# A graph layer: masks and inverse roots on VectorE instead of GpSimd, per-node work behind the second product

## The chip, the cores and the metric

One core of a Trainium2 chip. The metric is device microseconds of one execution, the median of the runs in the fast state; all runs of this study were in that state but one of b_order, 468.86 us, which the record marks as slow and which is left out. The kernel before takes 458 us. Engines: PE is TensorE, DVE is VectorE, ACT is ScalarE, POOL is GpSimd.

## The reference, cut to what matters

Two graph layers over N = 3327 nodes of 64 features, with a dense 0/1 adjacency matrix in fp32:

```python
h = jnp.maximum(_layernorm(x), 0.0)
x = x + gnn_0(h, adj)       # for every pair (i, j): sigmoid * adj * logmap(h_i, h_j), summed over j;
                            # then for every node: expmap, proj
h = jnp.maximum(_layernorm(x), 0.0)
mask = (adj != 0)
rank = jnp.cumsum(mask, axis=1)             # how many neighbours lie behind j
w = mask * where(pos > 0, 0.5 ** (k - pos), 0.0)
x = x + (w @ (h @ weight) + bias)
# ... (the hyperbolic functions are cut)
```

The first layer costs one 3327 x 3327 set of pair products. The second needs a running count of neighbours over the same matrix, so both are done in one sweep. Between them lies a stage on each node alone: three inverse roots, one tanh and some sixty operations on 4 to 8 values in each partition, a dozen more on 256 to 512.

## The kernel before

The sweep has four strips of columns, of 8, 8, 6 and 4 blocks of 128 nodes, in 91 rounds (26, 26, 26 and 13). One round, in the order of the program:

```python
STRIPS = [(0, 8), (8, 8), (16, 6), (22, 4)]
ON_ACT = ((1, 5), (4, 7), (2, 3), (1, 2))    # share of the reads of pc that ACT takes, by strip
PORTIONS, LAST = (2, 5, 5, 16), 6            # node-stage work let through in a round, by strip; LAST: behind a decode
BIG, LATER = 4, 99                           # a wide instruction counts 4, a small one 1
# ...
            total(n - 2)                                        # PE: sum of the products, fp32
            A.activation(pq, pq, AF.Gelu, scale=-WG / QS)       # ACT: two passes over the pair products
            A.activation(pq, pq, AF.Gelu, scale=WH)
            # ...
            V.scalar_tensor_tensor(sg, sg, 1.0, ad_of.pop(n)[:, :w], op0=ALU.add, op1=ALU.mult)  # "first product"
            edges(m + 1)            # the mask: G.tensor_scalar(mask, ad, 0.0, None, op0=ALU.is_equal)
            count(m, js(m)[-1])     # PE: neighbour count from the masks, into pc
            sigmoids(n + 1)         # ACT
            read(m, js(m)[-1])      # pc -> 8 bits, by ACT or by DVE
            products(n + 1)         # PE: pair products, into pq
            advance(PORTIONS[k])    # a portion of the node stage of the strip before
            if lo == 0:
                for _ in steps:     # last round of a strip: whatever is left of it
                    pass
            # ...
            V.scalar_tensor_tensor(sg, pq, WD, sg, op0=ALU.add, op1=ALU.mult)                    # "second product"
```

The node stage is a generator: each `yield` says what it just issued counts for. Its roots start on POOL, then take one refining step on DVE:

```python
G.tensor_tensor(y, v, nhalf[:, :n], op=ALU.pow)
V.tensor_scalar(g, v, -0.5, None, op0=ALU.mult)
yield LATER
# ... three dependent DVE instructions
```

Behind the sweep comes the tail: 26 decodes of the counts ("wt", alternately DVE and ACT), the products of the second layer on them, and, in portions behind the decodes, the node stage of the last strip. The products of the last four blocks need its result.

## Time and profile before

The median is 458.52 us (457.63 to 458.9, 3 runs). By stages, cut at the first "first product" of each strip and at DVE's copy-out of the last strip's sums:

| start | strip 0 | strip 1 | strip 2 | strip 3 | tail |
|---|---|---|---|---|---|
| 47.2 us | 89.3 | 106.6 | 87.0 | 61.2 | 65.1 |

Two of the rows by slices, each digit the busy tenths of a fortieth of the span:

```profile
DVE  4893899999999799998999999999889999789821
POOL 8910699887897697695968787959877541014000
```

DVE is full almost to the end. POOL's digits are high too, but a busy engine is a bound only if another waits for it.

### The profile page before, as it was taken

Reading aid. Unit: us, or ns where it says so; the run is one execution under the profiler, and the core shown is the slowest. Engines: PE = TensorE matmul, PEld = TensorE weight load, DVE = VectorE, ACT = ScalarE, POOL = GpSimd, SP = SyncE. Lnnn points to the kernel's source line nnn. Section 1 sums busy time; section 2 is a strip of 40 time slices with the busy share of each in tenths; the row PEclk is TensorE's granted clock in tenths of the full one; section 3 lists DMA queues with packets and bytes.
Section 4 is the critical chain, followed back from the end, with each engine's and each line's share of the span. In section 5 each row is a group of like instructions: output and inputs, shape, how many; then the busy total and the mean of one; then the engine's idle time right before and its main releaser. Section 6 shows DMA issues by size and latency. Waiting matters only on the chain.

```text
span 456.4 us, 4831 instructions
## 1 busy us (share of the span) xinstructions
PE 368.4 (81%) x1460; PEld 155.6 (34%) x1460; DVE 393.1 (86%) x660; ACT 369.9 (81%) x399; POOL 289.7 (63%) x137
## 2 busy tenths in 40 slices
PE   0336799999998989879889988698778689678973
PEld 0034233333333323323334444343332232233453
DVE  4893899999999799998999999999889999789821
ACT  1647989999999899887899999779798689577930
POOL 8910699887897697695968787959877541014000
PEclk9997999999998999998999999989899899999987
DMA  7402455545555343444236444336443100000002
GB/s 201 201 12 62 136 157 170 166 141 155 154 194 157 110 130 105 143 130 138 73 102 182 119 123 136 103 106 175 146 124 102 53 1 0 1 0 1 1 21 62
DMA packets 23313, 48.98 MB, mean 107 GB/s; under 512 B 8713, under 2 KB 9169, under 8 KB 23279
## 3 DMA queue, kind: packets, MB, share of 16 engines
q1 hardware_dynamic: 20993, 47.66, 35.0%
q10 hardware_dynamic: 2062, 0.87, 0.9%
q0 software_dynamic: 224, 0.07, 0.3%
q8 instruction: 13, 0.21, 0.2%
q14 instruction: 21, 0.17, 0.1%
HBM read 46.40 MB, written 0.87 MB: 104 GB/s over the span
## 4 chain that ended last, share of the span: by engine, by line
PE 34%; DVE 32%; ACT 20%; issue 7%; DMA 2%; POOL 2%; DVEq 0%; ACTq 0%; POOLq 0%
PE po L993 14%; DVE sg L1077 8%; DVE sg L1058 7%; ACT pq L1048 4%; PE pq L983 4%; ACT wt L1100 4%; ACT sg L976 4%; PE pq L984 4%; PE pc L956 4%; PE pc L955 4%; ACT pq L1049 3%; PE pw L1107 2%; DVE behind_lo L969 2%; DVE behind_hi L969 2%; DMA w_lr<-in_w_att 2%
## 5 line engine op out<-in xcount | busy, mean ns | idle before, releaser
L944 POOL TENSOR_SCALAR mask<-ad 128x1024 bf16<-128x1024 f32 (+1 forms) x91 | 254.5, 2801 | 81.9 <-PE pc L955 57.8
L993 PE MATMUL po<-sg,hw 128*65 128x512 f32 (+1 forms) x364 | 161.7, 568 | 1.6 <-DVE sg L1077 1.3
L1058 DVE SCALAR_TENSOR_TENSOR sg<-sg,ad 128x1024 f32<-128x1024 f32 (+1 forms) x91 | 112.6, 1237 | 6.6 <-ACT sg L976 6.5
L1077 DVE SCALAR_TENSOR_TENSOR sg<-pq,sg 128x1024 f32<-128x1024 f32 (+1 forms) x91 | 103.8, 1141 | 2.7 <-ACT pq L1049 1.5
L1048 ACT ACTIVATE pq<-pq 128x1024 f32<-128x1024 f32 (+1 forms) x91 | 86.7, 952 | 20.3 <-PE pq L984 14.9
L976 ACT ACTIVATE sg<-left_b,right 128x1024 f32<-128x1024 f32 (+2 forms) x104 | 100.5, 980 | 0.0
L1049 ACT ACTIVATE pq<-pq 128x1024 f32<-128x1024 f32 (+1 forms) x91 | 86.2, 947 | 2.9
L955 PE MATMUL pc<-mask,ca 128*128 128x512 bf16 (+1 forms) x175 | 66.5, 380 | 23.4 <-DVE behind_hi L969 8.3
L983 PE MATMUL pq<-iu,ju 71*128 71x512 f16 (+1 forms) x182 | 68.7, 377 | 17.0 <-DVE sg L1077 16.3
L956 PE MATMUL pc<-mask,cb 128*128 128x512 bf16 (+1 forms) x182 | 67.7, 382 | 12.6 <-POOL mask L944 11.1
L993 PEld LDWEIGHTS po<-sg,hw 128*65 128x65 f32 x364 | 49.9, 139 | 72.8 <-issue 56.4
L984 PE MATMUL pq<-iz,jz 128*128 128x512 f16 (+1 forms) x182 | 67.5, 378 | 3.8 <-DMA iz<-jz 3.8
L1107 PE MATMUL pw<-wt,s 128*128 128x512 bf16 (+1 forms) x182 | 40.4, 371 | 10.2 <-ACT wt L1100 7.0
L956 PEld LDWEIGHTS <-cb 128*128 128x128 bf16 x182 | 18.2, 100 | 74.2 <-issue 54.3
L969 DVE TENSOR_SCALAR behind_hi<-pc,none 128x1024 uint8<-128x1024 f32 (+2 forms) x26 | 28.2, 1084 | 6.9 <-PE pc L956 6.7
L969 DVE TENSOR_SCALAR behind_lo<-pc,none 128x1024 uint8<-128x1024 f32 (+2 forms) x26 | 29.0, 1115 | 5.1 <-ACT pq L1049 2.6
L967 ACT ACTIVATE behind_hi<-pc,none 128x1024 uint8<-128x1024 f32 (+2 forms) x26 | 24.6, 945 | 8.0 <-PE pc L956 7.9
L983 PEld LDWEIGHTS <-ju 71*128 71x128 f16 x182 | 18.3, 100 | 36.8 <-DVE sg L1077 18.0
L967 ACT ACTIVATE behind_lo<-pc,none 128x1024 uint8<-128x1024 f32 (+2 forms) x26 | 23.9, 919 | 7.8 <-PE pc L956 7.8
L517 POOL TENSOR_TENSOR rn<-t,nhalf 128x8 f32<-128x8 f32 (+2 forms) x8 | 13.7, 1709 | 25.1 <-DVE t L770 22.4
L984 PEld LDWEIGHTS <-jz 128*128 128x128 f16 x182 | 18.3, 101 | 31.2 <-issue 12.0
L1107 PEld LDWEIGHTS <-s 128*128 128x128 f16 x182 | 17.8, 100 | 30.3 <-issue 11.6
(227 smaller groups left out, 302.7 us busy)
## 6 DMA issues: line engine op xcount, KB each, us to landing
ad<-in_adj_t SPq DMA_DIRECT2D x65, 512.0 KB, 3.6
ad<-in_adj_t SPq DMA_DIRECT2D x26, 384.0 KB, 3.2
out<-o SPq DMA_DIRECT2D x6, 128.0 KB, 1.9
left_b<-left_d SPq DMA_DIRECT2D x1, 512.0 KB, 4.7
x_sb<-in_x ACTq DMA_DIRECT2D x1, 416.0 KB, 5.7
x_sb<-in_x SPq DMA_DIRECT2D x1, 416.0 KB, 5.0
left_b<-left_d SPq DMA_DIRECT2D x1, 384.0 KB, 4.1
iz<-jz ACTq DMA_DIRECT2D x2, 128.0 KB, 2.3
```

Source lines behind the costliest of these rows:

```text
L944: G.tensor_scalar(*args, 0.0, None, op0=ALU.is_equal)
L955: T.matmul(S.pc[:, f0:f1], ca, S.before[:, f0:f1], start=False, stop=True, skip_group_check=True)
L956: T.matmul(S.pc[:, f0:f1], cb, now[:, f0:f1], start=S.first, stop=True, skip_group_check=True)
L969: V.tensor_scalar(kept, S.pc[:, : S.F], rest, 0.0, op0=ALU.add, op1=ALU.max)
L976: A.activation(part(n, sg, j), S.left[:, : S.F], AF.Tanh, bias=right[:, j : j + 1], scale=0.5)
L983: T.matmul(part(n, pq, j, f0, f1), ju[:KB, j, :], S.iu[:, f0:f1], start=True, stop=False)
L984: T.matmul(part(n, pq, j, f0, f1), jz[:, j, :], S.iz[:, f0:f1], start=False, stop=True)
L993: T.matmul(S.po[: D + 1, f0:f1], hw[:, j, :], part(n, sg_of[n], j, f0, f1), start=j == NB - 1, stop=j == 0)
L1048: A.activation(pq, pq, AF.Gelu, scale=-WG / QS)
L1049: A.activation(pq, pq, AF.Gelu, scale=WH)
L1058: V.scalar_tensor_tensor(sg, sg, 1.0, ad_of.pop(n)[:, :w], op0=ALU.add, op1=ALU.mult)
L1077: V.scalar_tensor_tensor(sg, pq, WD, sg, op0=ALU.add, op1=ALU.mult)
```

## The change

The intent: take the masks off POOL, whose work disturbs DVE through the memory port that the two share; keep the node stage in one place; and let PE have the second product sooner, by placing the node stage's portion behind it. To pay for the masks on DVE, ACT takes more of the reads. The diff, cut to its core:

```diff
-ON_ACT = ((1, 5), (4, 7), (2, 3), (1, 2))
+ON_ACT = ((1, 2), (5, 8), (3, 4), (1, 2))
-PORTIONS, LAST = (2, 5, 5, 16), 6
+PORTIONS, LAST = (2, 4, 4, 8), 8
 # ... masks: 1 where there is an edge, so the counting weights change sign and a bias tile goes
-        G.tensor_scalar(*args, 0.0, None, op0=ALU.is_equal)
+        V.tensor_scalar(*args, 0.0, None, op0=ALU.not_equal)
-            V.tensor_scalar(kept, S.pc[:, : S.F], rest, 0.0, op0=ALU.add, op1=ALU.max)
+            V.tensor_scalar(kept, S.pc[:, : S.F], 0.0, None, op0=ALU.max)
 # ... each root: 11 dependent DVE instructions instead of POOL's power and 4 on DVE
+        for _ in range(3):
+            E.tensor_mul(t, y, y)
+            E.scalar_tensor_tensor(t, v, -0.5, t, op0=ALU.mult, op1=ALU.mult)
+            E.scalar_tensor_tensor(y, t, 1.5, y, op0=ALU.add, op1=ALU.mult)
 # ... ACT's three steps of the node stage wait for the next round, behind its Gelus
+            asked_of_act()
 # ... the portion behind the second product
-            advance(PORTIONS[k])
-            if lo == 0: ...
-            V.scalar_tensor_tensor(sg, pq, WD, sg, op0=ALU.add, op1=ALU.mult)
+            if hi - lo > 1:
+                advance(PORTIONS[k])
+            V.scalar_tensor_tensor(sg, pq, WD, sg, op0=ALU.add, op1=ALU.mult)
+            advance(PORTIONS[k])
+            if lo == 0: ...
```

The node stage has 76 small DVE instructions in the new form, 59 in the old. The new code also holds an unused branch ("hidden") that puts these small instructions on POOL in another form.

## The prediction

> **What bounds the kernel now.** I read the page first, then the instructions by form, then the busy time of each engine in five stretches cut at the first "sg<-sg,ad" of each strip, then the instructions in order of time. The page's first rows give two engines near the span and POOL far below it; its groups show the work that the change moves:
>
> ```profile
> PE 368.4 (81%) x1460; PEld 155.6 (34%) x1460; DVE 393.1 (86%) x660; ACT 369.9 (81%) x399; POOL 289.7 (63%) x137
> ...
> L944 POOL TENSOR_SCALAR mask<-ad 128x1024 bf16<-128x1024 f32 (+1 forms) x91 | 254.5, 2801 | 81.9 <-PE pc L955 57.8
> ...
> L1058 DVE SCALAR_TENSOR_TENSOR sg<-sg,ad 128x1024 f32<-128x1024 f32 (+1 forms) x91 | 112.6, 1237 | 6.6 <-ACT sg L976 6.5
> L1077 DVE SCALAR_TENSOR_TENSOR sg<-pq,sg 128x1024 f32<-128x1024 f32 (+1 forms) x91 | 103.8, 1141 | 2.7 <-ACT pq L1049 1.5
> ```
>
> POOL spends 254.5 us on 91 masks but idles 81.9 us ahead of them, mostly for PE to free a mask buffer: POOL has room, so taking the masks from it gains nothing by itself. An average over stages hides the rest, hence the stretches (strips 0, 1, 2, 3 and the tail, in this order):
>
> ```profile
> core 0: us, PE busy (x) PEld busy (x) DVE busy (x) ACT busy (x) POOL busy (x), PEclk, DMA share, GB/s
> 47.20:136.50 89.30, 86.31 (x299) 32.77 (x299) 85.34 (x81) 83.86 (x84) 77.08 (x26) 1.00 0.53 161
> 136.50:243.14 106.64, 95.23 (x319) 35.13 (x318) 99.49 (x136) 95.14 (x99) 80.27 (x32) 0.97 0.43 126
> 243.14:330.11 86.97, 74.24 (x315) 34.12 (x314) 80.80 (x136) 77.44 (x103) 70.66 (x32) 0.96 0.46 131
> 330.11:391.30 61.19, 48.74 (x156) 17.49 (x154) 54.36 (x109) 49.05 (x67) 30.03 (x14) 0.97 0.19 56
> 391.30:456.40 65.10, 46.50 (x240) 25.03 (x240) 43.55 (x103) 40.75 (x21) 8.25 (x4) 0.93 0.07 15
> ```
>
> Strip 0 runs 26 rounds in 89.3 us, 3.43 us each. In order of time its matmuls follow each other without a gap: 16 of them, 0.215 us apart, make 3.45 us. PE sets that strip. Strip 1 has the same matmuls per round but takes 4.10 us; DVE is busy 99.5 of 106.6 us there and carries the per-node stage of strip 0. Strips 2 (3.35 us a round) and 3 look alike: DVE sets strips 1 to 3. In the tail ACT's last decode ("wt") ends at 436.8 us and the last products wait for it.
>
> Part of DVE's time in strips 1 to 3 is lost, not worked:
>
> ```profile
> 159.60 1.00 DVE L757 TENSOR_TENSOR t<-sa,hv 128x8 f32<-128x8 f32 x1
> 160.63 0.17 DVE L759 TENSOR_TENSOR u<-u,t 128x8 f32<-128x8 f32 x1
> 162.34 2.09 DVE L1058 SCALAR_TENSOR_TENSOR sg<-sg,ad 128x1024 f32<-128x1024 f32 x1
> 167.15 1.22 DVE L1058 SCALAR_TENSOR_TENSOR sg<-sg,ad 128x1024 f32<-128x1024 f32 x1
> ```
>
> The same form takes 0.17 or 1.00 us, 1.22 or 2.09 us, the long ones while POOL works on a mask; after POOL's last mask no long one is left. Summing each form's excess over its undisturbed duration gives 11.4 us in strip 1 (9 first products, 7 small ones, one wide one), 9.4 in strip 2 and 2.2 in strip 3. DVE's real gaps (over 0.3 us) are 5.5, 4.1 and 5.3 us.
>
> **What the Trainium skill says.** "VectorE: DVE Perf Modes", The perf-mode tier table: an fp32 tensor_scalar from SBUF runs at 2 elements a cycle, a two-tensor fp32 operation and anything from PSUM at 1. The trace agrees on a neighbour: the decode takes 1.89 us for 3328 elements, the first product 1.22 us for 1024. "SBUF — State Buffer", SBUF: two separate sides: DVE and GpSimd share a port pair, taken by a DVE operation with two SBUF inputs or in a 2-port mode. The trace agrees that such operations are the disturbed ones (the second product, with one input in PSUM, never is), but the loss is at most 0.9 us, not the whole 2.99 us of a mask. "GPSIMD Engine Reference", 1. Specifications, names the same sharing. So the change does buy back the 23 us.
>
> **The change, part by part.** Starts of undisturbed DVE instructions lie 1.13 us apart for 1024 elements (1067 ns of elements and 63 ns), 0.86 for 768, 0.20 for a small one that needs the one before, some 0.1 for one that does not.
> - Masks: estimate, from the 2-a-cycle row and the 63 ns: 512/0.96 + 63 = 0.60 us for 1024, 0.46 for 768. Strip 0: 26 x 0.60 = 15.6; strip 1: mostly 1024, 15.6; strip 2: 22 x 0.46 + 4 x 0.60 = 12.5; strip 3: 9 x 0.60 = 5.4; four fall before the loop.
> - Reads of "pc": by the built order DVE does 13 instead of 20 in strip 0, 9 for 11 in strips 1 and 2, each 0.06 us shorter without its pointer operand. -8.7 us in strip 0, -2.9, -2.4, -0.3 after it. ACT takes them at about 0.95 each.
> - Per-node stage: three roots of 11 dependent instructions instead of 4, some others fused: 76 small instructions instead of 59, +17 x 0.2 = +3.4 us for each of the four node groups.
> - The portions: at four small or one wide instruction a round, 26 rounds don't suffice. In the built order strips 1 and 2 end with a flush of 18 DVE instructions in one round, with two round trips to ACT inside (Square, then the copy): 0.9 us each, 1.8 a strip.
> - Later placement of the portions lets the second product run earlier. Where DVE is the bound this moves a wait but removes no work; I credit 2, 1.5 and 2 us of gaps in strips 1 to 3.
>
> Sums. Start: masks +2.4, port losses before the loop -2.7, fewer instructions: -1. Strip 0: DVE 26 x (1.13 + 1.13 + 0.60) + 13 x 1.13 + 2 = 91; ACT 26 x 3.0 + 13 x 0.95 = 90; PE 89.3; three engines level, so +2. Strip 1: -11.4 - 2.9 + 15.6 + 3.4 - 2 + 1.8 = +4.5. Strip 2: -9.4 - 2.4 + 12.5 + 3.4 - 1.5 + 1.8 = +4.4. Strip 3: -2.2 - 0.3 + 5.4 + 3.4 - 2 = +4.3.
>
> Tail: ACT is the one to follow:
>
> ```profile
> 401.71 0.20 ACT L777 ACTIVATE k<-t 128x4 f32<-128x4 f32 x1 [2.62 <-DVE t L775]
> 401.83 11.56 ACT L1100 ACTIVATE wt<-behind_lo 128x3328 uint16<-128x3328 uint8 x4
> 413.30 2.96 ACT L1100 ACTIVATE wt<-behind_hi 128x3328 uint16<-128x3328 uint8 x1
> 418.81 0.42 ACT L856 ACTIVATE dt<-w 128x256 f32<-128x256 f32 x1 [2.55 <-DVE w L854]
> ```
>
> ACT waits 2.6 us at each of the per-node steps. In the built order of the changed kernel Tanh stands behind three decodes (two before), Square behind seven (as before), the copy behind eight (nine before), so five decodes follow it instead of four. Counting DVE's instructions from its first decode, Tanh's input is there at 10.9 us (no wait on ACT), Square's at 29.2 where ACT is free at 22.6 (6.6 us idle), the copy's at 34.9 where ACT is free at 32.5; five decodes of 2.87 then end at 49.6 instead of 44.9: +4.7.
>
> Total: -1 + 2 + 4.5 + 4.4 + 4.3 + 4.7 = +18.9, 477 us. I go to 475, because small losses under 0.3 us, not counted above, also go with POOL's masks.
>
> **Rivals.** (1) The port theory is worth more than I count, and the earlier second product feeds PE so well that strips 1 to 3 fall toward PE's 3.45 us a round. For it: PE idles in strip 1 and waits for DVE's second product are in the list of waits. Against it: DVE then needs 105 us of work for 26 rounds whatever the order. It would give 445 to 458. (2) Even trade: masks cost what the port gave back, flush and tail hide in slack: 458 to 465. Against it: masks add 49 us inside the loop, port and reads return 37, of which 8.7 in a strip that PE bounds anyway. (3) The mask does not get the fast mode, because its output is narrower than its input: 1.13 instead of 0.60, +48 us, 520. Against it: the decode, 8 to 16 bits, is fast. (4) DVE busy in strip 0 now stalls PE by turns, as rounds with a DVE read need 4.0 us and those with an ACT read cost ACT 3.9: 3.7 us a round, 5 us more: 480.
>
> **Range and chances.** Between rival 2 and rival 4 plus a worse tail: 463 to 487. Faster by over 2% (below 449.3) would need rival 1 nearly whole: 0.05. Within 2% (to 467.7) needs half of the sum to be wrong: 0.20. Slower: 0.75.
>
> **What would show it.** Mask on DVE at 0.69 us each; first product at 1.22 us throughout and no small instruction near 1 us; rounds of 3.5, 4.25, 3.5 and 5.0 us in strips 0 to 3; DVE busy over 95% in strips 1 and 2; a flush at the end of both; ACT waiting over 5 us for the Square of the last nodes, with its last decode some 5 us later after the loop than before. I am wrong if masks are shorter than 0.6 us, if strips 1 and 2 run under 4.0 and 3.3 us a round, or if the tail stays at 65 us.

## The result, and the profile after

The changed kernel takes 477.64 us (475.17 to 478.32, 4 runs) against 458.07 (456.79 to 458.9, 4 runs) of the kernel before. The ratio is 1.042, with a 95% interval from 1.0374 to 1.0466: slower. Ratios here are the mean time of one kernel's fast runs over that of the other's in the same rounds, so not quite the ratio of the medians quoted. Executions over 1.5% slower than the fastest of the same kernel are left out of the means. The prediction was right in direction and within 3 us in size.

The page's rows that answer to the first ones in the prediction; the columns of the groups are count, busy us, mean ns and idle time just before with its releaser:

```profile
PE 376.5 (79%) x1438; PEld 158.8 (33%) x1460; DVE 413.3 (87%) x807; ACT 373.7 (79%) x410; POOL 12.0 (3%) x33
...
L1075 DVE SCALAR_TENSOR_TENSOR sg<-sg,ad 128x1024 f32<-128x1024 f32 (+1 forms) x91 | 103.6, 1138 | 6.7 <-ACT sg L981 6.7
L1090 DVE SCALAR_TENSOR_TENSOR sg<-pq,sg 128x1024 f32<-128x1024 f32 (+1 forms) x91 | 103.5, 1138 | 6.2 <-ACT pq L1065 6.0
...
L950 DVE TENSOR_SCALAR mask<-ad 128x1024 bf16<-128x1024 f32 (+1 forms) x91 | 58.7, 646 | 0.0
```

POOL is down to 12 us. The first product, 1237 ns before, is now exactly as long as the second, 1138. A mask costs 646 ns on DVE where POOL took 2801. And yet DVE is 20 us busier. In the order of time, a stretch of strip 1 that answers to the one with the long instructions in the prediction:

```profile
168.87 0.17 DVE L755 TENSOR_TENSOR t<-sa,hv 128x8 f32<-128x8 f32 x1
169.07 0.17 DVE L755 TENSOR_TENSOR u<-u,t 128x8 f32<-128x8 f32 x1
169.15 1.22 DVE L1075 SCALAR_TENSOR_TENSOR sg<-sg,ad 128x1024 f32<-128x1024 f32 x1
```

The instruction that took 1.00 us takes 0.17, and no first product of this size exceeds 1.23 us in the whole trace (before: up to 2.09). So the mechanism that the change aimed at is real and gone. The five stretches (strips 0 to 3, tail; columns as in the prediction):

```profile
48.35:139.09 90.74, 88.36 (x297) 33.49 (x301) 90.60 (x100) 89.07 (x91) 0.00 (x0) 0.98 0.52 159
139.09:249.23 110.14, 97.47 (x323) 36.28 (x327) 103.57 (x177) 95.27 (x101) 1.41 (x2) 0.96 0.41 125
249.23:341.36 92.13, 75.98 (x305) 34.75 (x309) 84.90 (x178) 77.80 (x106) 1.42 (x2) 0.91 0.42 122
341.36:406.56 65.20, 50.62 (x145) 17.79 (x147) 59.08 (x136) 47.34 (x66) 2.06 (x2) 0.88 0.17 49
406.56:476.00 69.44, 46.07 (x236) 24.90 (x240) 45.76 (x120) 40.85 (x21) 0.72 (x1) 0.93 0.06 14
```

The third number of each row is DVE's busy time. In strip 1 it grew from 99.49 to 103.57 us in spite of 11 us of port losses gone; DVE idles 6.6 us there, 7.2 before. The same in strip 2 (80.80 to 84.90) and strip 3 (54.36 to 59.08). The column PEclk, the mean clock that TensorE was granted as a share of full speed, fell too: 0.91 and 0.88 in strips 2 and 3, 0.96 and 0.97 before. In strip 0 PE, DVE and ACT are now all within 2.4 us of the stage's length.

The tail, in ACT's order of time:

```profile
417.91 0.20 ACT L809 ACTIVATE k<-t 128x4 f32<-128x4 f32 x1 [0.68 <-DVE t L755]
...
435.33 0.42 ACT L863 ACTIVATE dt<-w 128x256 f32<-128x256 f32 x1 [5.75 <-DVE w L860]
435.66 2.96 ACT L1120 ACTIVATE wt<-behind_hi 128x3328 uint16<-128x3328 uint8 x1
440.96 0.40 ACT L874 CAST s<-w 128x256 f16<-128x256 f32 x1 [2.34 <-DVE w L871]
441.27 14.44 ACT L1120 ACTIVATE wt<-behind_hi 128x3328 uint16<-128x3328 uint8 x5
```

The bracket is ACT's idle time before the instruction. ACT waits 5.75 us for the Square's input and 2.34 for the copy's; before it waited 2.55 and nothing at these two. Its last decode ends at 455.7 us, 49.1 after the tail's start; before, 45.4.

### The profile page after: what moved, and what is told of

It reads as the page before. It is cut to its first block, busy times and chain, and to the rows that moved or that the text cites. A ratio compares the mean times of both kernels' runs of the same rounds, so it can differ in the third digit from the quotient of the medians.

```text
span 476.0 us, 4753 instructions
## 1 busy us (share of the span) xinstructions
PE 376.5 (79%) x1438; PEld 158.8 (33%) x1460; DVE 413.3 (87%) x807; ACT 373.7 (79%) x410; POOL 12.0 (3%) x33
## 4 chain that ended last, share of the span: by engine, by line
## 5 line engine op out<-in xcount | busy, mean ns | idle before, releaser
L998 PE MATMUL po<-sg,hw 128*65 128x512 f32 (+1 forms) x364 | 165.7, 580 | 0.8 <-DVE sg L1090 0.5
L1075 DVE SCALAR_TENSOR_TENSOR sg<-sg,ad 128x1024 f32<-128x1024 f32 (+1 forms) x91 | 103.6, 1138 | 6.7 <-ACT sg L981 6.7
L961 PE MATMUL pc<-mask,ca 128*128 128x512 bf16 (+1 forms) x169 | 65.0, 385 | 37.6 <-ACT behind_hi L972 13.3
L962 PE MATMUL pc<-mask,cb 128*128 128x512 bf16 (+1 forms) x170 | 64.3, 388 | 16.0 <-DVE mask L950 15.4
L950 DVE TENSOR_SCALAR mask<-ad 128x1024 bf16<-128x1024 f32 (+1 forms) x91 | 58.7, 646 | 0.0
L972 ACT ACTIVATE behind_hi<-pc 128x1024 uint8<-128x1024 f32 (+2 forms) x31 | 27.0, 872 | 13.5 <-PE pc L962 13.5
L972 ACT ACTIVATE behind_lo<-pc 128x1024 uint8<-128x1024 f32 (+2 forms) x32 | 27.4, 857 | 10.6 <-PE pc L962 10.0
L961 PEld LDWEIGHTS <-ca 128*128 128x128 bf16 x175 | 17.9, 103 | 31.4 <-issue 20.5
L974 DVE TENSOR_SCALAR behind_hi<-pc 128x1024 uint8<-128x1024 f32 (+2 forms) x21 | 20.8, 988 | 3.5 <-ACT sg L981 1.3
L1120 ACT ACTIVATE wt<-behind_hi 128x3328 uint16<-128x3328 uint8 x7 | 20.4, 2961 | 0.0
```

What stands on the lines that cost most here:

```text
L950: V.tensor_scalar(*args, 0.0, None, op0=ALU.not_equal)
L961: T.matmul(S.pc[:, f0:f1], ca, S.before[:, f0:f1], start=False, stop=True, skip_group_check=True)
L962: T.matmul(S.pc[:, f0:f1], cb, now[:, f0:f1], start=S.first, stop=True, skip_group_check=True)
L998: T.matmul(S.po[: D + 1, f0:f1], hw[:, j, :], part(n, sg_of[n], j, f0, f1), start=j == NB - 1, stop=j == 0)
```

## The experiments

Twelve runs were made, all with correct results. They are edits of the kernel before ("b_") or of the changed one ("a_" and "best"); one, a_again, is the changed kernel unedited. The calls were three, with the kernel before timed in each: 458.06, 458.64 and 458.69 us. The second call (a_portions5, a_last7, a_reads_as_before, a_nodes_pool) ran on another chip than the other two.

**Theory.** POOL's masks cost DVE some 23 us through the port; masks on DVE cost more than that, the additional reads on ACT pay for the difference, and the 20 us come from the node stage: 17 more small instructions for each strip, a flush of leftovers in the last round, and a worse tail. **Rivals:** the masks themselves are the loss; or the order is what matters, in either direction.

### The control

The changed kernel again.

> The changed kernel once more, as a control on the chip of this call. If the small edits' surplus gains (the shorter tail's kernel 3.5 us under its estimate, the smaller portions' 3.5 us under theirs) are effects of the edits, this comes out at 476 to 479 us. If it comes out at 474 or less, a part of both was only the variation from call to call.

It took 474.76 us (473.86 to 475.82), ratio 1.035 (1.0302 to 1.0397). This is 2.9 us less than the first time, in between the two readings that were written down. So a difference of 3 us between calls says nothing here, and the edits of the changed kernel are read against both 477.6 and 474.8. By stages the control's strips 1 and 2 were 1.5 and 1.4 us shorter, the tail nearly the same, 69.3.

The record shows what most of this variation goes with: over the eight runs of the changed kernel the time falls from 478.3 us at a mean granted clock of 0.937 to 473.9 at 0.950, some 3 us for each 0.01. In the two traces the 1.5 us of strip 1 lie in one round, of 5.39 us the first time and 3.92 in the control; just ahead of it the clock record shows half speed for 6.83 us the first time and 3.41 in the control. The clock is also a rival that no experiment here held fixed: the kernel before ran at 0.954 to 0.967, b_masks_reads below at 0.965 to 0.971, the changed kernel at 0.936 to 0.950. At 3 us for each 0.01, an estimate from those eight runs, the 0.02 between b_masks_reads and the control would be some 6 of the 18 us between them.

### Is the shared port real, and what is it worth?

The masks back on POOL in the changed kernel (with "is_gt", which gives the same on 0/1 data):

```diff
-        V.tensor_scalar(*args, 0.0, None, op0=ALU.not_equal)
+        G.tensor_scalar(*args, 0.0, None, op0=ALU.is_gt)
```

> The changed kernel with its 91 masks back on POOL, all else as changed. Work theory (DVE sets strips 1 to 3; a mask costs it 0.60 us and the port loss comes back): strip 1 110.1 - 15.6 + some 13 of port loss = 108, strip 2 92.1 - 12.5 + 11 = 91, strip 3 65.2 - 5.4 + 2.5 = 62, strip 0 at PE's 89.5, tail unchanged at 69: total some 468 (464 to 472), with first products of 2 us and small instructions near 1 us again. Rival, order theory (placement, flush and late ACT steps cost, the masks are innocent): 475 or more. Rival, masks alone: 456 to 462.

472.87 us (472.48 to 475.04), ratio 1.0317: a little above its own range, well above what "the masks alone" would give. Taking back the change's title item returns 2 to 5 us of 20. The stages missed in both directions: strip 1 took 104.5 us where 108 was expected, strip 2 97.4 where 91 was.

The opposite dose: the masks stay on DVE, and POOL gets a useless instruction of the same kind each round.

```diff
         V.tensor_scalar(*args, 0.0, None, op0=ALU.not_equal)
+        junk = work.tile([P, FMAX], U8, name="junk", bufs=1)
+        G.tensor_scalar(junk[:, : span(n)], ad_of[n][:, : span(n)], 0.0, None, op0=ALU.is_gt)
```

> The changed kernel, and POOL compares every adjacency tile once more into a tile that nobody reads. DVE's instruction list is the same. Port theory (what stretched DVE's instructions before was POOL at work): first products of 2 us and small instructions near 1 us come back, masks on DVE stretch too: +20 to +45 us, 498 to 523. Rival (the long durations came from waits or transfers, not from POOL): within 4 us of 477.6.

515.92 us (513.98 to 518.76), ratio 1.127: inside the range, 38 to 41 us more, from work whose result nobody uses. The two rows of the mask of 1024, in the loaded kernel and, in the fence behind it, in the changed one:

```profile
L950 DVE TENSOR_SCALAR mask<-ad 128x1024 bf16<-128x1024 f32 x65 | 66.7, 1027 | 0.0
```

```profile
L950 DVE TENSOR_SCALAR mask<-ad 128x1024 bf16<-128x1024 f32 x65 | 44.3, 683 | 0.0
```

The same instruction is stretched from 683 to 1027 ns in the mean, at most to 1.55 us. Over the whole trace DVE's masks inside the sweep took 26 us longer, its small instructions 10, the start 7. The page "SBUF — State Buffer" of the Trainium skill, SBUF: two separate sides, counts both kinds (two inputs in SBUF; a fast mode that uses two ports) among those that meet GpSimd at the port, and this agrees. So a mask on DVE and steady work on POOL are a bad pair: the mask itself becomes one of the disturbed.

### Masks and reads alone

In the kernel before, only the mask's engine:

```diff
-        G.tensor_scalar(*args, 0.0, None, op0=ALU.is_equal)
+        V.tensor_scalar(*args, 0.0, None, op0=ALU.is_equal)
```

> The kernel before with its masks on DVE, all else as before. Work theory: strip 0 becomes DVE's, 26 x 2.86 + 20 x 1.2 = 98.4 plus some 2, +11 us; strip 1 -11.4 + 15.6 = +4; strip 2 -9.4 + 12.5 = +3; strip 3 -2.2 + 5.4 = +3; tail +0: total some 479 (474 to 484), with no long first products. Order theory: at or under 462, as the masks are said to be innocent. Even-trade rival (port loss returns all that the masks cost): 456 to 463.

470.13 us (469.51 to 472.12), ratio 1.0271: 9 us better than expected. Strip 0 grew by 11.4 us, as expected: without the reads' help DVE outlasts PE there. Strips 1 to 3 changed by +1.2, -1.5 and +2.2 us, less than masks minus port losses should have cost. What was missed: DVE's gaps over 0.3 us in strips 1 and 2 went from 5.5 and 4.1 us to 2.9 and none. The opposite corner is the changed kernel with the reads shared as before:

```diff
-ON_ACT = ((1, 2), (5, 8), (3, 4), (1, 2))
+ON_ACT = ((1, 5), (4, 7), (2, 3), (1, 2))
```

> The changed kernel with the share of reads that ACT had before (DVE does 20, 11 and 11 of them in strips 0, 1 and 2 instead of 13, 9 and 9). Work theory: with its masks DVE is the bound of strip 0 too, so +7 x 1.13 = +8 there, +2.3 and +1.7 in strips 1 and 2: some 490 (486 to 494). Rival (ACT is level with DVE and what it loses of reads it gives back as earlier products): 476 to 481.

489.76 us (487.96 to 491.47), ratio 1.068, as expected: strip 0 takes 99.6 us instead of 90.7. With the masks on DVE, ACT's share of the reads is worth 12 to 15 us. Then both edits together in the kernel before, everything else old:

```diff
-ON_ACT = ((1, 5), (4, 7), (2, 3), (1, 2))
+ON_ACT = ((1, 2), (5, 8), (3, 4), (1, 2))
-        G.tensor_scalar(*args, 0.0, None, op0=ALU.is_equal)
+        V.tensor_scalar(*args, 0.0, None, op0=ALU.is_equal)
```

> The kernel before with the masks on DVE and with the changed kernel's share of the reads of pc on ACT, nothing else: per-node stage, its roots on POOL, its place ahead of the second product, portions and ACT's order stay as before. My theory (masks and reads are an even trade, the loss is the per-node stage's): the masks alone gave 470; the reads give back the 10 us of strip 0 and about 2 us in each of strips 1 and 2, so about 456 us (453 to 460). Rival (the masks are what costs, whatever the reads do): 466 or more.

456.42 us (454.36 to 457.54), ratio 0.9949 (0.9898 to 1.0001), as expected. This is the central run: masks and reads are an even trade, a gain of about half a per cent (by the interval, none to one), and the change's net loss lies in the rest of it and in what that rest brings with it. Its strips 1 to 3:

```profile
138.48:240.88 102.40, 91.95 (x318) 33.83 (x317) 101.23 (x161) 95.98 (x101) 6.37 (x5) 1.00 0.43 130
240.88:326.83 85.95, 74.62 (x314) 34.45 (x313) 82.88 (x160) 78.25 (x105) 7.16 (x5) 0.96 0.46 136
326.83:389.67 62.84, 49.05 (x156) 17.45 (x154) 57.55 (x117) 49.19 (x67) 5.13 (x5) 0.97 0.17 51
```

DVE is busy 101.23 of 102.40 us in strip 1: 1.2 us idle, against 7.2 in the kernel before, 6.6 in the changed one and 5.0 in the control. The same in strip 2: 3.1, against 6.2, 7.2 and 6.0. Strip 1 of this trace also had the full clock (1.00), which none of the other three had (0.96 to 0.97), so part of its small idle time may be the clock's.

### The order

In the kernel before, only the portion moved behind the second product:

```diff
+            V.scalar_tensor_tensor(sg, pq, WD, sg, op0=ALU.add, op1=ALU.mult)
+            if ended:
+                strip_out(k - 1)
             advance(PORTIONS[k])
             # ...
-            if ended:
-                strip_out(k - 1)
-            V.scalar_tensor_tensor(sg, pq, WD, sg, op0=ALU.add, op1=ALU.mult)
```

> The kernel before with only the placement changed: portions and the copy of the ended strip go behind the second product. Work theory: in strips 1 to 3 DVE does the same work in another order, so the time is 455 to 461. Order rival 1 (the earlier second product feeds PE and strips 1 and 2 fall toward 3.45 us a round): under 450. Order theory (the placement is what makes the changed kernel slower): over 463.

461.84 us over its three fast runs (460.92 to 462.97), ratio 1.0094 (1.0014 to 1.0173), a little above the range. An earlier second product buys nothing by itself. What it costs shows in DVE's idle time just ahead of the second product, 12.4 us here against 2.7 in the kernel before (its line is in the prediction):

```profile
L1071 DVE SCALAR_TENSOR_TENSOR sg<-pq,sg 128x1024 f32<-128x1024 f32 (+1 forms) x91 | 104.1, 1144 | 12.4 <-ACT pq L1049 7.9
```

The trace of the changed kernel shows how such a wait comes about. A round early in strip 1, in the changed kernel:

```profile
156.50 0.68 DVE L950 TENSOR_SCALAR mask<-ad 128x1024 bf16<-128x1024 f32 x1
159.03 1.23 DVE L1090 SCALAR_TENSOR_TENSOR sg<-pq,sg 128x1024 f32<-128x1024 f32 x1 [1.84 <-ACT pq L1065]
160.17 0.68 DVE L788 TENSOR_REDUCE vv<-u 128x8 f32<-128x512 f32 x1
```

and the same part of strip 1 in the kernel with masks and reads alone:

```profile
155.46 0.68 DVE L944 TENSOR_SCALAR mask<-ad 128x1024 bf16<-128x1024 f32 x1
156.07 0.16 DVE L746 TENSOR_TENSOR sa<-sa,su 128x8 f32<-128x8 f32 x1
...
156.62 1.22 DVE L1077 SCALAR_TENSOR_TENSOR sg<-pq,sg 128x1024 f32<-128x1024 f32 x1
```

In the second, node-stage work stands ahead of the second product, and the wait for ACT's Gelu disappears behind it. In the first, DVE comes to the second product at once, waits 1.84 us for ACT with its node-stage work queued behind the wait, and does that work afterwards. Its length here is not typical: in the control the same wait is 0.37 us, and the round is the one behind the half clock described under "The control". On an engine that works in program order, work that is ready belongs in front of a wait. How much of the changed kernel's idle time comes from this placement and how much from ACT's later steps was not separated: placement alone, in the kernel before, left DVE's idle time in strip 1 at 7.0 us, as it was, and raised it in strips 2 and 3 from 6.2 and 6.8 to 7.4 and 8.4. The next run shows that the larger part of it in strips 1 and 2 is the flush's.

### The flush

Portions of 5 instead of 4 in strips 1 and 2, so that nothing is left for the last round:

```diff
-PORTIONS, LAST = (2, 4, 4, 8), 8
+PORTIONS, LAST = (2, 5, 5, 8), 8
```

> The changed kernel with five portions a round instead of four in strips 1 and 2, so that the per-node stage ends inside its strip; the built order shows no flush. Flush theory: the two round trips to ACT inside each flush (0.70 and 0.68 us of DVE idle in the trace, twice) go, DVE's work stays: some -3 us, 474.6 (472.5 to 476.5). Rival 1 (the flush also drains PE and ACT and costs the rounds after it): 470 or less. Rival 2 (hidden): 477 or more.

471.12 us (469.55 to 471.48), ratio 1.0264 (1.0221 to 1.0307): better than its range, 6.5 us below the first time of the changed kernel, 3.6 below the control. Strips 1 and 2 took 107.1 and 88.7 us; the changed kernel took 110.1 and 92.1 at first, 108.7 and 90.7 as the control. So the flush costs 1.6 to 3.4 us a strip. The wait of DVE for ACT inside it is visible in the changed kernel's trace:

```profile
340.75 0.69 DVE L876 TENSOR_TENSOR s<-w,s 128x512 f16<-128x512 f32 x1 [0.68 <-ACT s L874]
```

A second one of 0.70 us stands ahead of it, for the Square; together 1.4. DVE's whole idle time fell from 5.0 and 6.0 us in the control's strips 1 and 2 to 3.0 and 3.6.

The flush has a second effect, which my theory lacked. Behind the flush of strip 1, whose last round takes 10.2 us where a_portions5 has 3.3, the changed kernel's trace shows TensorE at half its clock (0.50 in the row, whose columns are those of the stretches), its matmuls 0.43 us apart instead of 0.22:

```profile
248.20:261.80 13.60, 7.95 (x26) 3.91 (x27) 11.45 (x16) 11.63 (x18) 0.00 (x0) 0.50 0.35 96
```

All six traces with this flush (the changed kernel twice, a_masks_pool, a_idle_pool_loaded, a_reads_as_before and a_last7) have a stretch of 13.65 us at half clock at the end of strip 1 and one of 6.83 to 10.24 us at the end of strip 2; of the eight others none has more than 3.41 us within 8 us of these ends. So the half clock comes with the flush. What it costs was not separated from the waits: PE is busy in only 7.95 of these 13.60 us.

### The tail

One portion less behind each late decode, which puts one decode fewer behind the copy:

```diff
-PORTIONS, LAST = (2, 4, 4, 8), 8
+PORTIONS, LAST = (2, 4, 4, 8), 7
```

> The changed kernel with seven instead of eight portions behind each decode of the tail. By DVE's instruction times ACT's Square then stands behind eight of its decodes and its copy behind ten, so three decodes follow the copy instead of five. Tail theory: ACT's last decode ends some 3.9 us earlier: 473.7 (472 to 475.5), ACT's wait for Square down from 5.75 to some 3 us. Rival (the end is set by PE's products or by the transfers out, not by ACT's last decode): 477 or more.

468.56 us (467.71 to 470.25), ratio 1.0209 (1.0167 to 1.025): 5 us better than expected against the first time of the changed kernel, 6.2 us below the control. The tail fell from 69.4 to 63.8 us; the last decode ends 45.4 us after the tail's start instead of 49.1, about the 3.9 earlier that were expected. ACT's wait for the Square fell to 4.35 us, not to 3. ACT's end of the tail:

```profile
440.90 0.39 ACT L874 CAST s<-w 128x256 f16<-128x256 f32 x1
441.19 8.71 ACT L1120 ACTIVATE wt<-behind_hi 128x3328 uint16<-128x3328 uint8 x3
```

No bracket at the copy: one more decode stands ahead of it, fills the 2.34 us of idle time, and only three follow. Both edits together:

```diff
-PORTIONS, LAST = (2, 4, 4, 8), 8
+PORTIONS, LAST = (2, 5, 5, 8), 7
```

> The changed kernel with portions of 5 instead of 4 in strips 1 and 2 (no instructions left over for the last round) and 7 instead of 8 late decodes on ACT. If both single edits' gains are real and lie in different stages they add: 477.6 - 6.5 - 9.1 = about 462 us (460 to 467). If the part of the tail edit's gain that lay outside the tail (3.5 us) was variation: about 467.

465.26 us (464.71 to 465.75), ratio 1.0151: inside the range, 9.5 us under the control, where the two alone gave 3.6 and 6.2. The two repairs of placement add up. The control stood 16.1 us above the kernel before; 6.6 are left. That is of the size of the additional work: 17 small instructions at 0.20 us make 3.4 us in each of strips 1 to 3 by my estimate, less the 2.3 us that masks and reads gain.

### The node stage's small instructions, and a faster kernel

The unused branch switched on for the nodes of strips 0 to 2, whose node stage runs inside the sweep; the last strip's, in the tail, stays on DVE:

```diff
-        hidden = False
+        hidden = b0 < STRIPS[-1][0]
```

> The changed kernel with the small per-node instructions of strips 0 to 2 on POOL, which the changed kernel leaves idle; the last strip's stay on DVE. Work theory: DVE loses 76 small instructions, some 12 us, in each of strips 1 to 3, and the 1.4 us of the flush waits: 110 to 97, 92 to 79, 65 to 57, tail and strip 0 as they are: some 443 (438 to 450). Rival (POOL's small instructions take the port again and again and give the gain back): 458 or more.

453.32 us (451.62 to 454.56), ratio 0.9872 (0.9825 to 0.9919): 21 to 24 us less than the changed kernel, but 10 more than I expected. DVE has 579 instructions instead of 807. It waits for POOL where I had assumed it would not, 3.2 to 4.3 us in each of strips 1 to 3, the first of them:

```profile
190.10 0.69 DVE L849 TENSOR_TENSOR w<-h,t 128x512 f32<-128x512 f32 x1 [3.18 <-POOL t L755]
```

The chain on POOL ahead of it has some instructions of 0.20 us, but also powers of 1.67 us and others of over 1 us. The trace shows what holds these others: DVE. For example, in strip 1:

```profile
181.97 0.69 DVE L950 TENSOR_SCALAR mask<-ad 128x1024 bf16<-128x1024 f32 x1
182.19 0.53 POOL L755 TENSOR_TENSOR t<-t,t 128x8 f32<-128x8 f32 x1
```

Of 34 such instructions of over 0.4 us, powers left out, 33 overlap a first product or a mask of DVE, and 32 of these end 0.04 to 0.11 us after it; of the 155 quick ones 17 overlap one. Over 0.20 us each, the 34 lose 29.5 us, so the rival had a point, with the sides exchanged: DVE takes the port from POOL. The last kernel does not cure this (39 slow ones, all of them overlapping); it gives the chain more rounds, and takes the tail's repair too:

```diff
-PORTIONS, LAST = (2, 4, 4, 8), 8
+PORTIONS, LAST = (2, 8, 8, 8), 7
-        hidden = False
+        hidden = b0 < STRIPS[-1][0]
-        yield from after(4)
+        yield from after(6 if nb > 6 else 5)
```

> An attempt to beat both kernels: the changed kernel with the per-node stage's small instructions of strips 0 to 2 on POOL (that alone gave 453.3), portions that leave nothing over, slots that give POOL a round more before DVE needs its result, and 7 late decodes on ACT. From 453.3: about 5.5 us less in the tail, about 3 us less waiting of DVE for POOL in each of two strips and 2 in the third: about 441 us (437 to 447). If POOL's own pace is what DVE waits for, whatever the slots, only the tail's part comes: 448 or more; 451 or more if not even that.

439.29 us (438.86 to 440.41), ratio 0.9589 (0.9548 to 0.9631): 4.1% faster than the kernel before, 7.5 to 8% faster than the changed one, and inside its range. Its strips 1 to 3:

```profile
138.26:236.84 98.58, 93.21 (x316) 35.28 (x315) 94.01 (x101) 93.14 (x100) 34.30 (x68) 0.97 0.45 134
236.84:318.09 81.25, 72.81 (x316) 34.13 (x315) 75.09 (x101) 77.51 (x106) 31.01 (x68) 0.98 0.48 142
318.09:373.14 55.05, 47.16 (x156) 16.94 (x154) 49.26 (x59) 47.65 (x67) 25.46 (x68) 1.00 0.20 62
```

In strip 1 PE, DVE and ACT are within 1 us of each other: so there relief for one of them alone should gain little; this was not tried. POOL's work is 34 us there instead of 80, in short instructions; only half a microsecond of stretched DVE masks is left in that strip. One wait for POOL remains, 3.10 us in strip 3.

## Why the prediction was right

The stages, with the kernel that has masks and reads alone in between; "control" is the changed kernel's second profile, all in us:

| stage | before | masks and reads | changed | control | changed - before | predicted | best |
|---|---|---|---|---|---|---|---|
| start | 47.2 | 46.9 | 48.3 | 48.5 | +1.1 | -1 | 47.5 |
| strip 0 | 89.3 | 91.5 | 90.7 | 90.8 | +1.4 | +2 | 90.7 |
| strip 1 | 106.6 | 102.4 | 110.1 | 108.7 | +3.5 | +4.5 | 98.6 |
| strip 2 | 87.0 | 86.0 | 92.1 | 90.7 | +5.2 | +4.4 | 81.2 |
| strip 3 | 61.2 | 62.8 | 65.2 | 65.7 | +4.0 | +4.3 | 55.1 |
| tail | 65.1 | 64.8 | 69.4 | 69.3 | +4.3 | +4.7 | 64.0 |
| span | 456.4 | 454.4 | 476.0 | 473.7 | +19.6 | +18.9 | 437.1 |

**Right, term by term.** The rounds were predicted at 3.5, 4.25, 3.5 and 5.0 us and came at 3.49, 4.24, 3.54 and 5.02 (stage over number of rounds). The mask was predicted at 0.69 us and measured 0.683. The estimate behind it, 0.60 us from a mask's start to the next instruction's, holds too: 0.60 in the trace with portions of 5, between starts at 339.78 and 340.38 us. DVE's busy time was to grow, by the sums without gaps and flush, by 4.7 us in strip 1 and grew by 4.1; in strip 2 by 4.1, and grew by 4.1. In the tail Square's wait was predicted at 6.6 us and was 5.75, the copy's at 2.4 and was 2.34.

**Right in sum, not in its cause.** The step "Later placement of the portions lets the second product run earlier", with its credit of 2, 1.5 and 2 us of gaps, is not borne out: b_order, with the placement alone, had no less idle time of DVE (7.0, 7.4 and 8.4 us in strips 1 to 3, before 7.2, 6.2 and 6.8). Masks on DVE did remove idle time: 4.1 and 1.3 us were left in strips 1 and 2 with them alone (b_masks_dve), 1.2 and 3.1 with the reads too. The rest of the change brought back 4 to 5 us of it in strip 1 and 3 to 4 in strip 2, of which the flush is 2.1 and 2.4 (the control against a_portions5). Credit and flush together were to change the idle time of strips 1 and 2 by -0.2 and +0.3 us; it changed by -0.6 and +1.1 the first time, by -2.1 and -0.1 in the control. So the sum came close partly by luck: two effects that the prediction did not have in this form cancel, and the granted clock, which it left out, moves the result by as much as its miss. Where the masks moved and the rest did not, in b_masks_dve, the same reckoning was 9 us too high.

**Wrong.** The start was to be 1 us shorter and was 1.1 longer. DVE's small instructions (up to 26 elements) did fall there, from 18.9 to 13.9 us, but the first wide reduction of the squares starts at 15.07 us instead of 13.29: three masks stand ahead of it in DVE's order, and a weight that DVE converts first landed 0.6 us later. I had added the masks' duration without asking what they delay. DVE's share in strips 1 and 2 was to be over 95%; it was 94.0 and 92.2%, in the control 95.3 and 93.4. The last decode was to come 4.7 us later after the tail's start and came 3.7 later; ACT also had a wait of 0.68 us at Tanh that I had not counted. In strip 3 DVE's busy time grew by 4.7 us, not by 6.3, and the idle time fell by 0.7, not by 2. Two lines were misread, without harm to a sum: PE's round is not 16 matmuls 0.215 us apart but 12, eight 0.217 us apart and four in fp32 0.428 apart, which make the same 3.45; and of ACT's three per-node steps in the tail before, Tanh and Square waited, the copy did not.

**The rivals.** Rival 1, the earlier second product feeds PE: falls with b_order, and with strips 1 and 2, which grew. Rival 2, an even trade: true of masks and reads, false of the whole. A rival that was not written down, the granted clock, may stand for some of the loss (see the control). Rival 3, no fast mode: falls with 683 ns. Rival 4, stalls by turns in strip 0: falls with 3.49 us a round.

## What to carry to other kernels

A change that mixes a relief with a rearrangement is to be priced in parts: here the relief was free (456.4 against 458.7 us), and the rest, more small instructions and the rearrangement, cost 18 us (474.8 against 456.4), some of it perhaps by the lower clock. On an engine that sets the pace, long chains of tiny instructions are the work to move away, to an engine that is idle anyway, with enough rounds for the slower chain to come back; long wide instructions there disturb the fast engine through the port (38 to 41 us here). On engines that work in program order, what is ready goes ahead of a wait, and leftovers are spread over the rounds rather than flushed at the end: the flush cost waits, and here half the clock for 13.65 us.

## What the Trainium skill lacked or had wrong

- "SBUF — State Buffer", SBUF: two separate sides, says that the loser at the shared port fully blocks for the other's whole instruction. With POOL as the loser the runs agree: its slow small instructions ended 0.04 to 0.11 us after DVE's in 32 of 33 cases. With DVE as the loser they show smaller losses: POOL's mask took 2.99 us in the mean, and the first product beside it at most 2.09 instead of 1.22; the DVE mask beside POOL's work at most 1.55 instead of 0.68. The losses are at most 0.9 us beside instructions recorded at 2.8 to 3.0 us in the mean; for how much of that POOL holds the port, no run shows.
- "VectorE: DVE Perf Modes", The TRN2 errata, gives two fixed terms for an instruction, 58 cycles in its table and about 150 in a remark that corrects it. Here both are right, for two things, by an estimate with the page's 0.96 GHz: the mask's recorded duration, 683 ns, is 533 ns of elements at 2 a cycle and 150 ns (144 cycles), near the second; the next instruction starts 0.60 us after it, 67 ns (64 cycles) more than the elements, near the first. The remark sets the second in place of the first, as if they were one quantity; one is the spacing, the other the duration.
- I found no page with the spacing of small DVE instructions of which each needs the one before. Here it is 0.20 us (168.87 to 169.07), where independent ones follow at 0.07 to 0.12. This difference sets the price of the roots.
- "GPSIMD Engine Reference", 3.1 Elementwise — side-by-side cycle accounting, gives costs for 512 and 2048 elements in a partition, none for a few. With 6 or 8, most took 0.20 us here and powers 1.34 to 2.02; the cheap ones that took more, up to 2.37, stood behind DVE (a_nodes_pool).
